# Where softmax's division is done in a cross-attention: after the values by transposed reciprocals, or on the exponentials ahead of their transposes

## The chip, the cores and the metric

The kernel runs on one core of a Trainium2 chip. The time is device time in microseconds from one execution of the whole program; several executions are made, and their median is compared. The profile is of one further execution.

## What is computed

The network has two layers on `x` (16 batches of 256 rows of 256 features) with a context of the same shape. Each layer is a cross-attention and a mixture of experts, each added to `x` after a layer norm. The change is in the second layer's cross-attention ("Layer 1" in the code, which counts from 0), 16 heads of 64:

```python
xn = _layernorm(x, ln_gamma, ln_beta)
q = (xn @ w_q).reshape(B, SQ, NUM_HEADS, DIM_HEAD)
k, v = jnp.split(context @ w_kv, 2, axis=-1)      # both (B, SK, heads, 64)
scores = jnp.einsum('bqhd,bkhd->bhqk', q * SCALE, k)
attn = jax.nn.softmax(scores, axis=-1)
out = jnp.einsum('bhqk,bkhd->bqhd', attn, v).reshape(B, SQ, INNER)
out = out @ w_out + b_out
return out * jnp.tanh(gate[0])
```

All is float32.

## The kernel before

Four stages follow each other: Layer 0's attention, its experts, Layer 1's attention (`layer1_attention`, L869), its experts. The page's lines are mostly L58, the line of the helper that records every instruction, so instructions are told apart by the tiles they name.

In Layer 1's attention a batch has 256 queries and 256 keys. The work is cut into units of two heads: eight units (`s` = 0 to 7) a batch, 128 in all. Of one unit, with `p` for the head, `lt` for the half of the queries and `mc` for the half of the keys:

- `l1_logits` (L938): four matmuls write `lg`; VectorE takes the maxima over keys, negated, into `nmx`, in two reductions.
- `l1_exp` (L956): ScalarE's exponentials, two for `lt` = 0 and two for `lt` = 1, write `ex` and add up the sums in `den`.
- `l1_transposes` (L974): eight TensorE transposes of `ex`, evicted into `exT` by VectorE (`mc` = 0) and ScalarE (`mc` = 1).
- `l1_sums` (L966): VectorE takes the reciprocals of the sums (`rden`); GpSimd spreads each over 64 columns (`wide`).
- `l1_scale` (L985): two TensorE transposes of `wide` into half of the bank `ov`, and a ScalarE copy of them into `scale`. Thus every output feature of a head has its queries' reciprocals in its own row.
- `l1_values` (L996): four matmuls of `exT` and the values into the other half of `ov`; VectorE multiplies by `scale` while it evicts into `oT`.

Logits and exponentials are of the current unit, and the others of the unit before it (`last`), which is one step behind.

Between these parts each step fills in pieces of other work, named in `places` by the unit's number: `p+1` is the next batch's projections (`l1_prepare`, L1050: keys, values, queries, and in unit 5 also the transposes of the normalised input, scaled into `xnT` by VectorE), `f-1` is the output projection of the batch before (`l1_finish`, L1121, in units 1 and 2, with the residual `up` and the statistics of the next norm), and `i+2` the input of the batch after the next (`l1_input`, L1013: gathers of the experts' outputs in unit 0, two additions and statistics in each of units 3 and 4, normalisation and more statistics in unit 5, the second normalisation in unit 6). A step has two fillers for TensorE, one ahead of the transposes and one behind them; the first is evicted by ScalarE and the second by VectorE (`self.side`). In the last batches, where no next batch is left, `choices` (L1176), the routing of the last stage, takes the place of `p+1`.

Every engine's instructions go out in the order in which the program names them (`in_order`, L105): an instruction that waits holds up all that is behind it on its engine. PSUM has two buffers for `lg`, three banks for `ps`, which transposes and projections take in turn, and one buffer for `ov`.

Of the kernel before, what the change touches and what calls it, by code (L numbers as in the profile page):

```python
# [8 lines left out]
F32 = mybir.dt.float32  # L9
I32 = mybir.dt.int32  # L10
AF = mybir.ActivationFunctionType
ALU = mybir.AluOpType
# [3 lines left out]
P = 128  # L16
B, S, D = 16, 256, 256
# [4 lines left out]
H = 16  # L22
DH0 = 16
DH1 = 64
# [39 lines left out]
class Net:  # L64
# [804 lines left out]
    def layer1_attention(self, mv2, mv3, late):  # L869
        nc, tc = self.nc, self.tc  # L870
        with ExitStack() as ctx:
            self.ps_lg = ctx.enter_context(tc.tile_pool(name="c_lg", bufs=2, space=PSUM, reuse_waits="tile"))
            self.ps = ctx.enter_context(tc.tile_pool(name="c_ps", bufs=3, space=PSUM, reuse_waits="tile"))
            self.ps_ov = ctx.enter_context(tc.tile_pool(name="c_ov", bufs=1, space=PSUM, reuse_waits="tile"))
            keep = ctx.enter_context(tc.tile_pool(name="c_keep", bufs=1, reuse_waits="tile"))
            self.work = ctx.enter_context(tc.tile_pool(name="c_work", bufs=2, reuse_waits="tile"))
            self.small = ctx.enter_context(tc.tile_pool(name="c_small", bufs=4, reuse_waits="tile"))

            self.pick_tiles(late)
            self.mv2, self.mv3 = mv2, mv3  # L880
            self.rs2 = keep.tile([P, NT], F32, name="ln2_rs")
            self.mvi, self.rsi = self.stats_tiles(keep, "ln2i")
            self.tg = keep.tile([P, 1], F32, name="tg")
            nc.scalar.activation(self.tg, self.gate, AF.Tanh)

            self.l1 = {b: {} for b in range(B)}
            pieces = {
                "i": {b: self.l1_input(b) for b in range(B)},
                "p": {b: self.l1_prepare(b) for b in range(B)},
                "f": {b: self.l1_finish(b) for b in range(B)},  # L890
            }
            nothing = iter(())

            places = (
                ("p+1", "p+1", "i+2"), ("f-1", "f-1", ""), ("f-1", "f-1", ""),
                ("p+1", "p+1", "i+2"), ("p+1", "p+1", "i+2"), ("p+1", "p+1", "i+2"),
                ("p+1", "p+1", "i+2"), ("p+1", "p+1", ""),
            )  # L900

            first = {0: "i+1", 1: "i+1", 2: "i+1", 3: "i+1 i+2", 4: "i+1 i+2"}
            choices = self.choices()

            def go_on(b, words):
                for word in words.split():
                    at = b + int(word[1:])
                    if word[0] == "p" and at >= B:

                        next(choices, None)  # L910
                    else:
                        next(pieces[word[0]].get(at, nothing), None)

            self.in_order()
            last = None
            for b in range(-1, B + 1):
                for s in range(H // 2):
                    one, two, chain = places[s]
                    if b < 0:
                        chain = first.get(s, "i+2")  # L920
                    self.l1_sums(last)
                    unit = self.l1_logits(b, s) if 0 <= b < B else None
                    self.l1_exp(unit, 0)
                    self.side = self.s
                    go_on(b, one)
                    self.l1_transposes(last)
                    self.l1_exp(unit, 1)
                    self.l1_scale(last)
                    go_on(b, chain)
                    self.side = self.v  # L930
                    go_on(b, two)
                    self.l1_values(last)
                    last = unit
            for _ in choices:
                pass
            self.any_order()
# [26 lines left out]
                bias=unit["nmx"][:, lt, p : p + 1], accum_out=unit["den"][:, lt, p : p + 1],  # L963
            )

    def l1_sums(self, unit):  # L966
        if unit is None:
            return
        rden = self.small.tile([P, 2, 2], F32, tag="rden", name="rden")
        self.v.reciprocal(rden, unit["den"])  # L970
        unit["wide"] = wide = self.small.tile([P, 2, 2, DH1], F32, tag="wide", name="wide", bufs=2)
        self.g.tensor_copy(wide, rden.unsqueeze(3).to_broadcast([P, 2, 2, DH1]))

    def l1_transposes(self, unit):  # L974
        if unit is None:
# [6 lines left out]
                    self.tp(tr[:, p, lt, :], unit["ex"][:, p, lt, ts(mc, P)])  # L982
            self.evac(exT[:, mc], tr.rearrange("p h t l -> p h (t l)"), on=(self.v, self.s)[mc])

    def l1_scale(self, unit):  # L985

        if unit is None:
            return

        unit["ov"] = ov = self.ps_ov.tile([P, 2, S], F32, tag="ov", name="ov")  # L990
        for lt in range(2):
            self.tp(ov[:, 1, ts(lt, P)], unit["wide"][:, lt].rearrange("p h d -> p (h d)"))
        unit["scale"] = scale = self.small.tile([P, S], F32, tag="scale", name="scale", bufs=2)
        self.s.copy(scale, ov[:, 1, :])

    def l1_values(self, unit):  # L996
        if unit is None:
            return
        t, s = self.l1[unit["b"]], unit["s"]
        if s == 0:  # L1000
            t["oT"] = []
        oT = self.work.tile([P, S], F32, tag="oT", name="oT", bufs=11)
        t["oT"].append(oT)
        ov, h0 = unit["ov"], 2 * s % (H // 2)
        for mc in range(2):
            for p in range(2):
                self.mm(
                    ov[ts(p, DH1), 0, :], t["vv"][2 * s // (H // 2)][:, mc, ts(h0 + p, DH1)],
                    unit["exT"][:, mc, p, :], start=(mc == 0), stop=(mc == 1),
                )  # L1010
        self.v.tensor_tensor(oT, ov[:, 0, :], unit["scale"], ALU.mult)

    def l1_input(self, b):  # L1013

# [465 lines left out]
```

## Time and profile before

| | us |
|---|---|
| median of 3 runs | 2285.07 |
| lowest and highest | 2281.6, 2285.92 |
| the profiled execution, its own time | 2289.61 |
| its span, first to last instruction | 2287.6 |
| Layer 1's attention, first logits to last | about 906 (1186 to 2092) |

The page gives the busy time of each engine, and for groups of instructions the mean time of one and what ended the idle time ahead of them. PE is TensorE's matmuls, PEld its weight loads (which run ahead of the matmuls and often show the wait), DVE is VectorE, ACT is ScalarE and POOL is GpSimd. In a timeline the columns are the start, the busy time, the engine, the line, the operation with the tiles it writes and reads, and in brackets the idle time of the engine just before with what ended it. Successive instructions of one kind stand as one row with their number; a matmul's listed time is longer than its distance to the next, since they are pipelined.

### The profile page before, as it was taken

What the parts mean: (1) busy time and instruction counts of PE and PEld (TensorE: products, weight loads), DVE (VectorE), ACT (ScalarE), POOL (GpSimd) and SP (SyncE); (2) the same over time, 40 slices, a digit from 0 to 9 for tenths busy, and PEclk for the clock granted to TensorE, in tenths of its full rate; (3) what the DMA queues carried; (4) which work ended last, traced back from release to release, by engine and by line L of the source; (5) the groups of instructions that cost most, each with busy time, mean ns of one, the idle gap of its engine ahead of it and who ended that gap; (6) DMA issues with size and microseconds to landing.
All of it is one profiled execution on the core that took longest, in us unless ns stands there. A gap on an engine that the chain in (4) does not pass through costs nothing. (4 is left out here: it accounts for less than half of the span.)

```text
span 2287.6 us, 40849 instructions
## 1 busy us (share of the span) xinstructions
PE 2138.9 (93%) x15742; PEld 1633.6 (71%) x15742; DVE 1169.1 (51%) x2692; ACT 920.7 (40%) x3092; POOL 399.2 (17%) x581
## 2 busy tenths in 40 slices
PE   6889989988589999999979999999999999998998
PEld 4666666666378998998856666666666666666887
DVE  4778787887510110110135555555555555547445
ACT  2656555555222222222214444444444444444432
POOL 2232333322300000000021111111111111016200
PEclk9999999999789999999989999999999999999999
DMA  9910000000077777777510000000000000002112
GB/s 371 422 45 13 19 15 15 19 12 18 25 231 251 251 231 255 249 229 259 173 33 10 10 10 10 10 10 10 10 10 10 10 10 10 1 1 85 32 39 75
DMA packets 129025, 200.42 MB, mean 88 GB/s; under 512 B 14480, under 2 KB 107040, under 8 KB 124480
## 3 DMA queue, kind: packets, MB, share of 16 engines
q1 hardware_dynamic: 120880, 176.14, 22.7%
q0 software_dynamic: 7136, 21.12, 2.8%
q8 instruction: 124, 2.03, 0.4%
q14 instruction: 69, 0.57, 0.1%
q10 hardware_dynamic: 816, 0.56, 0.1%
HBM read 142.35 MB, written 55.44 MB: 86 GB/s over the span
## 5 line engine op out<-in xcount | busy, mean ns | idle before, releaser
L58 ACT ACTIVATE ex<-lg,nmx 128x256 f32<-128x256 f32 x1024 | 473.9, 476 | 723.9 <-DVE nmx L58 723.8
L58 DVE TENSOR_REDUCE nmx<-lg 128x2 f32<-128x512 f32 x512 | 329.0, 685 | 110.6 <-PE lg L58 109.0
L58 PE MATMUL tr<-ident,ex 128*128 128x128 f32 x2048 | 280.0, 278 | 26.0 <-DVE exT L58 24.2
L58 PEld LDWEIGHTS tr<-ident,ex 128*128 128x128 f32 x2048 | 237.2, 143 | 77.6 <-DVE exT L58 41.1
L796 ACT ACTIVATE hT<-ph,b 128x256 f32<-128x256 f32 (+1 forms) x368 | 131.7, 423 | 367.9 <-issue 290.5
L58 PE MATMUL ph<-xT,w 128*128 128x256 f32 (+1 forms) x1472 | 257.9, 334 | 0.8 <-DVE xT L779 0.8
L58 PE MATMUL py<-w,hT 128*128 128x256 f32 x1136 | 252.8, 379 | 0.0
L58 PEld LDWEIGHTS ph<-xT,w 128*128 128x128 f32 x1472 | 232.1, 192 | 23.6 <-DVE xT L779 1.2
L58 DVE COPY exT<-tr 128x512 f32<-128x512 f32 x256 | 169.5, 683 | 130.6 <-PE tr L58 130.6
L58 PEld LDWEIGHTS py<-w,hT 128*128 128x128 f32 x1136 | 212.3, 190 | 27.0
L58 PE MATMUL lg<-kT,qT 32*128 32x256 f32 (+1 forms) x2048 | 224.1, 410 | 1.7 <-ACT ex L58 1.7
L58 PE MATMUL ov<-exT,vv 128*32 128x256 f32 (+1 forms) x2048 | 215.5, 399 | 7.1 <-ACT scale L58 5.2
L58 ACT ACTIVATION_READ_ACCUMULATOR ex<-lg,nmx 128x1 f32 x1024 | 212.0, 207 | 0.0
L58 POOL COPY wide<-rden 128x256 f32<-128x256 f32 x160 | 63.7, 398 | 821.5 <-DVE rden L58 462.5
L58 PEld LDWEIGHTS lg<-kT,qT 32*128 32x128 f32 (+1 forms) x2048 | 137.5, 190 | 87.5 <-issue 77.2
L58 PEld LDWEIGHTS ov<-exT,vv 128*32 128x32 f32 (+1 forms) x2048 | 90.7, 124 | 102.9 <-ACT scale L58 48.6
L58 POOL DMA_INDIRECT yg<-ys,row_out x64 | 62.7, 980 | 518.6 <-PE mm L58 497.7
L58 ACT ACTIVATE exT<-tr 128x512 f32<-128x512 f32 x256 | 147.3, 608 | 14.2 <-PE tr L58 12.3
L779 DVE COPY xT<-tr 128x512 f32<-128x512 f32 (+1 forms) x46 | 26.2, 570 | 242.0 <-PE tr L58 242.0
L811 DVE TENSOR_TENSOR yo<-py,b 128x512 f32<-128x512 f32 (+1 forms) x46 | 26.2, 570 | 226.0 <-PE py L58 208.4
L58 PE MATMUL mm<-xnT,w_q 128*128 128x256 f32 x512 | 129.3, 397 | 6.1 <-DVE xnT L58 6.1
L58 PE MATMUL mm<-w_kv,ctxT 128*128 128x512 f32 x256 | 127.5, 621 | 3.6 <-DVE vv L58 3.5
(201 smaller groups left out, 2697.7 us busy)
## 6 DMA issues: line engine op xcount, KB each, us to landing
w<-in_L_W SPq DMA_DIRECT2D x92, 1024.0 KB, 7.1
xs<-zero SPq DMA_DIRECT2D x4, 8192.0 KB, 52.6
xg<-xs SPq DMA_DIRECT2D x25, 256.0 KB, 5.5
ys<-yo SPq DMA_DIRECT2D x25, 256.0 KB, 6.8
b<-in_L_b SPq DMA_DIRECT2D x46, 128.0 KB, 4.2
x<-in_x SPq DMA_DIRECT2D x16, 256.0 KB, 6.0
ctxT<-in_ctxT SPq DMA_DIRECT2D x16, 256.0 KB, 6.0
w<-in_L_W1T SPq DMA_DIRECT2D x8, 512.0 KB, 9.1
```

The source lines that it names most:

```text
L58: self.last = f(*args, **kw)
L779: self.v.tensor_copy(s["xT"][:, :, 0 : s["rows"]], tr.rearrange("p c t l -> p c (t l)"))
L796: self.s.activation(s["hT"][:, h0 + j, 0:rows], ph[:, j, :], AF.Gelu, bias=s["b1"][:, h0 + j : h0 + j + 1],)
L811: self.v.tensor_tensor(yo[:, 0:nt, :], py, s["b2"].unsqueeze(1).to_broadcast([P, nt, D]), ALU.add)
```

## The change

The exponentials are divided by their sums before they are transposed. `l1_sums` and `l1_scale` are gone, and with them the tile `wide`, its two transposes and the copy `scale`. A new function, `l1_divide`, is called twice a unit, once for each half of the queries: VectorE takes the reciprocals of two sums and multiplies the two pieces of `ex` in place, each by its column. The values then need no scaling, and ScalarE copies them into `oT`.

```diff
-                    self.l1_sums(last)
                     unit = self.l1_logits(b, s) if 0 <= b < B else None
                     self.l1_exp(unit, 0)
                     self.side = self.s
                     go_on(b, one)
                     self.l1_transposes(last)
                     self.l1_exp(unit, 1)
-                    self.l1_scale(last)
+                    self.l1_divide(unit, 0)
                     go_on(b, chain)
+                    self.l1_divide(unit, 1)
                     self.side = self.v
                     go_on(b, two)
                     self.l1_values(last)
...
-    def l1_sums(self, unit):
+    def l1_divide(self, unit, lt):
+
         if unit is None:
             return
-        rden = self.small.tile([P, 2, 2], F32, tag="rden", name="rden")
-        self.v.reciprocal(rden, unit["den"])
-        unit["wide"] = wide = self.small.tile([P, 2, 2, DH1], F32, tag="wide", name="wide", bufs=2)
-        self.g.tensor_copy(wide, rden.unsqueeze(3).to_broadcast([P, 2, 2, DH1]))
+        rden = self.small.tile([P, 2], F32, tag="rden", name="rden")
+        self.v.reciprocal(rden, unit["den"][:, lt, :])
+        for p in range(2):
+            ex = unit["ex"][:, p, lt, :]
+            self.v.tensor_scalar(ex, ex, rden[:, p : p + 1], None, ALU.mult)
...
-    def l1_scale(self, unit):
...
-        unit["ov"] = ov = self.ps_ov.tile([P, 2, S], F32, tag="ov", name="ov")
-        for lt in range(2):
-            self.tp(ov[:, 1, ts(lt, P)], unit["wide"][:, lt].rearrange("p h d -> p (h d)"))
-        unit["scale"] = scale = self.small.tile([P, S], F32, tag="scale", name="scale", bufs=2)
-        self.s.copy(scale, ov[:, 1, :])
...
-        ov, h0 = unit["ov"], 2 * s % (H // 2)
+        ov, h0 = self.ps_ov.tile([P, S], F32, tag="ov", name="ov"), 2 * s % (H // 2)
...
-        self.v.tensor_tensor(oT, ov[:, 0, :], unit["scale"], ALU.mult)
+        self.evac(oT, ov, on=self.s)
```

More of the change, by code (lines that the diff above doesn't have):

```diff
@@ L983, in l1_transposes @@
             self.evac(exT[:, mc], tr.rearrange("p h t l -> p h (t l)"), on=(self.v, self.s)[mc])
-    def l1_scale(self, unit):
-        if unit is None:
-            return
-        unit["ov"] = ov = self.ps_ov.tile([P, 2, S], F32, tag="ov", name="ov")
-        for lt in range(2):
-            self.tp(ov[:, 1, ts(lt, P)], unit["wide"][:, lt].rearrange("p h d -> p (h d)"))
-        unit["scale"] = scale = self.small.tile([P, S], F32, tag="scale", name="scale", bufs=2)
-        self.s.copy(scale, ov[:, 1, :])
     def l1_values(self, unit):
@@ L1007, in l1_values @@
                 self.mm(
-                    ov[ts(p, DH1), 0, :], t["vv"][2 * s // (H // 2)][:, mc, ts(h0 + p, DH1)],
+                    ov[ts(p, DH1), :], t["vv"][2 * s // (H // 2)][:, mc, ts(h0 + p, DH1)],
                     unit["exT"][:, mc, p, :], start=(mc == 0), stop=(mc == 1),
                 )
-        self.v.tensor_tensor(oT, ov[:, 0, :], unit["scale"], ALU.mult)
+        self.evac(oT, ov, on=self.s)
     def l1_input(self, b):
```

## The prediction

> **What bounds the kernel now.** I read the page first, then the busy time by stretches, then the groups of instructions of the stretch that the change touches, and last the timeline of single units of that stretch.
>
> ```profile
> PE 2138.9 (93%) x15742; PEld 1633.6 (71%) x15742; DVE 1169.1 (51%) x2692; ACT 920.7 (40%) x3092; POOL 399.2 (17%) x581
> ```
>
> TensorE is the busy engine. The page's chain that ended last covers 3% of the span, so it can't carry an argument about Layer 1. One steady batch of Layer 1 lies between two projections of logits, at 1469.11 and 1525.68:
>
> ```profile
> 1469.11:1525.68 56.57, 56.56 (x327) 39.04 (x325) 33.16 (x72) 24.57 (x86) 9.00 (x16) 1.00 0.04 10
> ```
>
> In 56.57 us PE is busy throughout, VectorE for 33.16 and ScalarE for 24.57, at a granted clock of 1.00. This invites the thought that whatever leaves PE shortens the batch. The timeline of unit 6 (of 8, two heads each) says otherwise:
>
> ```profile
> 1511.51 1.13 PE L58 MATMUL lg<-kT,qT 64*128 64x256 f32 x8
> 1512.57 1.99 PE L58 MATMUL mm<-xnT,w_q 128*128 128x256 f32 x8
> 1512.69 1.29 DVE L58 TENSOR_REDUCE nmx<-lg 128x2 f32<-128x512 f32 x2 [0.49 <-PE lg L58]
> 1514.10 0.47 ACT L58 ACTIVATE ex<-lg,nmx 128x256 f32<-128x256 f32 x1 [4.34 <-DVE nmx L58]
> 1514.40 1.04 PE L58 MATMUL tr<-ident,ex 128*128 128x128 f32 x8
> 1515.01 0.59 ACT L58 ACTIVATE qT<-mm 128x512 f32<-128x512 f32 x1
> 1515.28 0.38 PE L58 MATMUL ov<-ident,wide 128*128 128x128 f32 x2
> 1515.65 1.59 PEld L58 LDWEIGHTS mm<-xnT,w_q 128*128 128x128 f32 x8 [0.23 <-ACT qT L58]
> 1515.65 1.99 PE L58 MATMUL mm<-xnT,w_q 128*128 128x256 f32 x8
> ```
>
> The two transposes of reciprocals (`ov<-ident,wide`) stand between the transposes of exponentials and the second projection, and the second projection waits for ScalarE's eviction of the first: of the three banks of `ps`, it takes the one that the eviction frees. From the logits to it: 1.18 to the maxima, 1.41 to the exponentials, 0.91 to the eviction, 0.64 to the projection, 4.14 us. PE's own work, 1.06 + 1.83 + 0.88 + 0.22, would be done at 3.99. Units 1 and 2, whose filler is the output projection (one bank, no eviction in between), show the transposes' true price:
>
> ```profile
> 1479.96 0.38 PE L58 MATMUL ov<-ident,wide 128*128 128x128 f32 x2
> ...
> 1480.18 1.89 PE L58 MATMUL mm<-w_out,oT 128*128 128x256 f32 x8
> ```
>
> There the next matmul starts 0.22 us after them, and the unit takes 6.82 instead of 7.08.
>
> **Part by part.** *Removed on PE: two transposes a unit.* The group's mean of 274 ns each is latency; start to start two cost 0.22. In units 0, 3, 4, 5, 6 and 7 they stand under the 4.14 us and are worth nothing; in 1 and 2, 0.22 each. [...]
>
> *Removed on ScalarE: the copy `scale` (0.39), replaced by the copy of `oT`* behind the values; ScalarE idles some 4 us a unit ahead of the exponentials (4.34 above), so this costs nothing. One thing is gained: the first exponential waits for two semaphores in the changed program where it waited for three. The trace's records of ScalarE have both forms: 117 ns from the end of the maxima with two held ahead of it (123 in Layer 1), 95 with one (48 in Layer 0). So 0.02 a unit on the 4.14 us chain.
>
> *Removed on GpSimd: `wide` (0.40).* Off the path in steady batches; it matters once, below.
>
> *Added on VectorE: two divides a unit, each a reciprocal and two 128x256 multiplications by a column in SBUF; removed: one reciprocal and the product `oT` (0.42).* The nearest rows are exact twins:
>
> ```profile
> 545.40 0.68 DVE L58 TENSOR_REDUCE first<-key 128x2 f32<-128x512 f32 x1
> 546.11 0.62 DVE L58 TENSOR_SCALAR hot<-rev,first 128x256 f32<-128x256 f32 x2
> 546.64 0.18 DVE L58 TENSOR_TENSOR r_one<-hits,r_row 128x32 f32<-128x32 f32 x1
> ```
>
> The pair behind a dependent small result starts 0.03 after it and holds the engine for 0.53 (546.64 - 546.11). One alone:
>
> ```profile
> L58 DVE TENSOR_SCALAR hot<-rev,first 128x256 f32<-128x256 f32 x32 | 9.9, 351 | 0.6
> ```
>
>  With the reciprocal (166 ns at 128x2, row `r_sm`) a divide occupies 0.17 + 0.03 + 0.53 = 0.74. The bounds of a multiplication: 0.18, what the 128x32 product above costs with hardly any elements in it, and 0.48 from the row `x<-yg,gates,x`, which works on the same 256 elements with a column as well. I take 351, the row of the same instruction.
>
> [...] The trace starts the second of a pair 0.27 after the first, though each is listed at 0.35. [...] The row is of this engine and this shape: I keep it.
>
> *Where the divides stand.* The first is behind the copy `exT`, the second behind the chain pieces. It waits for the sums of the second pair of exponentials (there 5.5 after the logits); behind it in VectorE's queue are the second eviction or the residual, and then the next maxima. The next unit's transposes wait for the divided tile, but only 2.9 after the next logits. Units 0 and 7: free long before the next maxima (at 6.9 of 8.26). Units 3 and 4: 4.13 (free behind `exT`) + 0.74 + 1.6 (chain: two adds, statistics) + 0.74 + 0.61 = 7.8, before the next maxima at 8.26. Units 1 and 2: the sums are there at 5.5; divide to 6.26, then residual and statistics, 1.54, to 7.8; the next maxima could start at 6.60 + 1.18 = 7.78. Just fits. Unit 5 doesn't:
>
> ```profile
> 1507.52 0.69 DVE L58 COPY exT<-tr 128x512 f32<-128x512 f32 x1 [1.05 <-PE tr L58]
> 1508.13 0.40 DVE L58 TENSOR_SCALAR xn<-x,ln_mv,ln_rs 128x256 f32<-128x256 f32 x1
> ...
> 1510.77 0.99 DVE L58 TENSOR_SCALAR xnT<-tr,gamma,beta 128x256 f32<-128x256 f32 x2
> ```
>
> From its logits (1504.00): `exT` lets go at 4.13, divide to 4.87, the two normalisations with statistics (1508.13 to 1510.11, 1.98) to 6.85, divide to 7.59, eviction `vv` 0.61 to 8.20, `xnT` twice 0.455 to 9.11. Unit 6's maxima start at 9.11 instead of 8.69 (1512.69), and its first projection, which reads `xnT`, at 9.25 instead of 8.57. Its second projection is then due by ScalarE at 9.11 + 1.41 + 0.91 + 0.64 - 0.02 = 12.05, by PE at 9.25 + 1.83 + 0.88 = 11.96; before, 11.65. Unit 6 loses 0.4.
>
> *Sum.* A batch: -0.44 (units 1, 2) + 0.40 (unit 6) - 0.02 x 5 = -0.14, 15 times -2.1; the last batch has no unit-5 work: -0.5. Start of Layer 1: in batch 0 the values wait for ScalarE's `scale` for 3.05 and 2.20 us; they now wait only for `exT`, 1.2 earlier each, but unit 1's maxima stand behind two divides and an eviction, 1.26 later: -1.1. First unit of the last batch: PE waits 2.66 for GpSimd's normalised `xn`, which stood behind `wide`; now VectorE's half is last, at 2037.6 instead of 2038.57, and the second piece gains a little too: -1.2. Last unit: 0.22 and a GpSimd wait of 0.36: -0.6. In the last batch GpSimd normalises beside the divides; VectorE's own `xn` there takes 0.49 where it takes 0.41 alone: +0.4. Total -5.1 on the profiled 2289.61 (span 2287.6, 2.0 around it). The median of the runs is 4.5 lower, and the same difference is taken from it: 2280.0.
>
> **Rivals.** *PE is the bound and all its busy time counts:* 0.38 x 128 = 49 us, 2236. For it: 93%. Against: the ScalarE wait at every second projection. 3% for that, 7% for a gain of 8 to 15, if unit 6 isn't late (-6 more) or the chains are shorter than drawn. *VectorE's multiplication is dearer, and unit 5 decides:* each 0.1 on it falls four times on unit 6's maxima, and twice on unit 3's, whose slack is gone. At 481 ns that is 0.13 x 6 = 0.8 a batch, 12 us, less the 5: 2292. It ends above before from 0.055 more per multiplication, that is at 0.41. [...] Against: the twin row's spread of 346 to 354. 30%; a tenth of that would end inside what a measurement can tell. *The change doesn't do what it says:* the built order has 256 transposes fewer on PE and 512 multiplications more on VectorE, so no.
>
> **Numbers.** The walk as drawn has 60%, with a spread of some 4 us: 2276 to 2284. A measurement tells about 0.2%, 4.6 us, from no change; the walk's -5 lies at that border, so it gives 0.33 to faster and 0.27 to the same; with 0.10 of the rivals that gain and the dear multiplication (0.03 the same, 0.27 slower) that makes 0.43, 0.30 and 0.27. The range goes from the late unit 6 not appearing, 2273, to the dear multiplication, 2292.
>
> **What would show it.** `ex<-ex,rden` at 0.35 us; unit 6 at 7.5 and units 1 and 2 at 6.6 us from logits to logits; the others at 7.06; second projections still waiting for ScalarE, now with PE idle 0.39; PE's busy share lower by about two points. Wrong if ordinary units fall under 6.9 (then the eviction didn't bound them), if `ex<-ex,rden` is over 0.41, or if units 3 and 4 get longer.

## The result, and the profile after

| | before | after |
|---|---|---|
| median of 6 runs, us | 2285.49 | 2277.68 |
| lowest and highest | 2281.6, 2287.57 | 2274.13, 2281.92 |
| profiled execution, its span | 2289.61, 2287.6 | 2274.13, 2271.7 |
| first to last logits of Layer 1's attention, profiled execution | 899.13 | 888.60 |

The ratio is 0.997, with a 95% interval of 0.9956 to 0.9985: between 3.4 and 10.1 us faster, 7.8 by the medians, where 5.1 was forecast. (The 906 given above for before ran to 2092; its last logits start at 2085.15.)

The two profiled executions differ by 15.9 us in span, which is not the change's worth. 5.9 of them lie ahead of Layer 1's first logits (1186.02 and 1180.16), in stages that the change doesn't touch; in all ten profiles of this study these logits stand between 1180.16 and 1186.2, and after has the earliest. From the first logits to the last after gains 10.53; behind them it loses 0.5. This last stage is untouched as well, apart from the last unit at its head, and it also varies, from 202.45 to 207.0 over the ten profiles. After's profiled execution is also the fastest of its six, and the granted clock goes with that. Its mean over an execution was 0.980 in this one and 0.976 in before's profiled one, while after's six average 0.977, as 39 later executions of before do. Among those 39, the six at 0.980 took 2280.03 to 2283.44 and the eight at 0.975 took 2287.78 to 2289.97: an estimate of 1.4 us for each 0.001. So the 7.8 of the medians is a gain at about equal clock, and the difference of the two traces isn't.

On the page of after, the engines' busy time and the row of the new instruction:

```profile
PE 2104.4 (93%) x15486; PEld 1598.0 (70%) x15486; DVE 1276.8 (56%) x3204; ACT 941.0 (41%) x3092; POOL 351.1 (15%) x453
...
L58 DVE TENSOR_SCALAR ex<-ex,rden 128x256 f32<-128x256 f32 x512 | 158.9, 353 | 9.1
```

TensorE lost 34.5 us of busy time (2138.9 to 2104.4), VectorE took on 107.7, and the kernel is some 8 us faster: neither number gives the third. A steady batch of after, from logits to logits, shows why; the columns are the stretch and its length, the busy time of PE, PEld, DVE, ACT and POOL, the granted clock, the DMA share and GB/s:

```profile
1458.39:1514.81 56.42, 54.92 (x310) 37.20 (x308) 39.91 (x104) 25.88 (x86) 5.97 (x8) 1.00 0.04 10
```

PE was busy for 56.56 of 56.57 before, and is now for 54.92 of 56.42: of 1.64 us less work 0.15 became time, and 1.49 became waiting. By units (logits to logits, from the timelines):

| unit | 0 | 1 | 2 | 3 | 4 | 5 | 6 | 7 | batch |
|---|---|---|---|---|---|---|---|---|---|
| before | 7.08 | 6.82 | 6.82 | 7.07 | 7.08 | 7.51 | 7.08 | 7.09 | 56.57 |
| after | 7.07 | 6.61 | 6.61 | 7.07 | 7.07 | 7.49 | 7.45 | 7.06 | 56.42 |

Units 1 and 2 gain their two transposes, the others nothing, and unit 6 loses 0.37. Unit 6 of after, in the timeline:

```profile
1500.29 1.13 PE L58 MATMUL lg<-kT,qT 64*128 64x256 f32 x8
1500.37 0.68 DVE L58 COPY vv<-mm 128x512 f32<-128x512 f32 x1
...
1500.97 0.98 DVE L58 TENSOR_SCALAR xnT<-tr,gamma,beta 128x256 f32<-128x256 f32 x2
1501.56 0.30 PEld L58 LDWEIGHTS mm<-xnT,w_q 128*128 128x128 f32 x2 [0.53 <-DVE xnT L58]
...
1501.88 1.27 DVE L58 TENSOR_REDUCE nmx<-lg 128x2 f32<-128x512 f32 x2
1502.01 1.16 PEld L58 LDWEIGHTS mm<-xnT,w_q 128*128 128x128 f32 x6 [0.16 <-DVE xnT L58]
...
1503.25 0.47 ACT L58 ACTIVATE ex<-lg,nmx 128x256 f32<-128x256 f32 x1 [2.46 <-DVE nmx L58]
```

The maxima carry no bracket: VectorE went to them straight from `xnT`. They start 1.59 after the logits, where an ordinary unit's start at 1.18, and the exponentials follow 1.37 behind them. In the ordinary units the eviction's wait is still there, with 0.20 where the prediction looked for 0.39:

```profile
1496.28 0.59 ACT L58 ACTIVATE vv<-mm 128x512 f32<-128x512 f32 x1
...
1496.92 0.30 PEld L58 LDWEIGHTS mm<-w_kv,ctxT 128*128 128x128 f32 x2 [0.44 <-ACT vv L58]
1496.92 1.98 PE L58 MATMUL mm<-w_kv,ctxT 128*128 128x512 f32 x4 [0.20 <-ACT vv L58]
```

(The bracket counts from the listed end of the transposes. They start at 1495.68, and in units 1 and 2 the next matmul follows 0.87 after their start; counted from there, PE waits 0.37.) The steady part gave only 1.9 us, over batches 1 to 14. The rest of the 10.53 is at the edges: 4.84 in batch 0 and 3.80 in the last batch.

**Start of Layer 1.** PE's rows of before, units 1 and 2 of batch 0:

```profile
1196.49 1.98 PE L58 MATMUL ov<-exT,vv 128*64 128x256 f32 x8 [3.05 <-ACT scale L58]
1198.39 2.08 PE L58 MATMUL lg<-kT,qT 64*128 64x256 f32 x8
...
1204.66 1.30 PE L58 MATMUL ov<-exT,vv 128*64 128x256 f32 x8 [2.20 <-ACT scale L58]
```

and of after, unit 2:

```profile
1191.31 1.13 PE L58 MATMUL lg<-kT,qT 64*128 64x256 f32 x8
1192.37 1.09 PE L58 MATMUL tr<-ident,ex 128*128 128x128 f32 x8
1194.52 0.65 PE L58 MATMUL ov<-exT,vv 128*64 128x256 f32 x4 [1.05 <-DVE exT L58]
```

The waits for `scale` are gone, as forecast; what is left are waits for the divided `ex` and for `exT`, of 0.80, 1.62 and 1.05. But the same eight matmuls of logits took 2.08 before and take 1.13. Units 1 and 2 as stretches, before and then after:

```profile
1190.73:1198.39 7.66, 4.61 (x27) 2.50 (x26) 2.64 (x5) 4.22 (x17) 0.39 (x1) 0.79 0.00 1
1198.39:1205.89 7.50, 5.30 (x28) 3.49 (x26) 2.40 (x5) 2.68 (x10) 0.40 (x1) 0.73 0.00 0
```

```profile
1184.88:1191.31 6.43, 3.66 (x26) 1.95 (x25) 4.73 (x13) 3.69 (x15) 0.00 (x0) 1.00 0.00 1
1191.31:1196.02 4.71, 3.39 (x27) 1.97 (x25) 3.45 (x9) 2.70 (x11) 0.00 (x0) 1.00 0.00 0
```

The granted clock (third column from the right) was 0.79 and 0.73, and is 1.00. The prediction had taken the rows' slow durations as fixed and moved only the wait.

But the shorter waits alone did not ensure the full clock. The kernel with unit 5 relieved (below) has the same instructions up to unit 5 of batch 0, and the same waits. In its profile the clock did fall, to one half for 6.82 us; two stretches, and the row with the longest wait:

```profile
1191.86:1195.28 3.42, 1.47 (x10) 0.87 (x8) 2.81 (x8) 0.68 (x5) 0.00 (x0) 1.00 0.00 0
1195.28:1202.10 6.82, 6.16 (x26) 3.50 (x28) 3.87 (x10) 3.50 (x13) 0.00 (x0) 0.50 0.00 0
```

```profile
1195.75 2.12 PE L58 MATMUL ov<-exT,vv 128*64 128x256 f32 x8 [1.63 <-DVE exT L58]
```

and in after it did not:

```profile
1185.37:1188.78 3.41, 1.93 (x14) 1.08 (x12) 2.79 (x8) 1.06 (x5) 0.00 (x0) 1.00 0.00 0
1188.79:1192.20 3.41, 2.13 (x16) 1.08 (x16) 2.21 (x8) 2.69 (x10) 0.00 (x0) 1.00 0.00 0
```

```profile
1189.72 0.65 PE L58 MATMUL ov<-exT,vv 128*64 128x256 f32 x4 [1.62 <-DVE exT L58]
```

These stretches are steps of 3.41 us, counted from a change of the clock (the last section): in the kernel with unit 5 relieved from the one at 1195.28, in after from the one at 1175.13. There, the wait of 0.80 and most of the 1.63 fell into one step, in which PE was busy for 1.47. Here, a step's end cut the long wait in two, and PE was busy for 1.93 and 2.13. Units 1 and 2 took 12.55 there and 11.14 here, so 1.4 of the 4.84 is luck of this execution.

**Last batch.** Its first unit waits for the normalised input of the last stage. The wait in PE's rows, in before and then in after:

```profile
2038.57 1.12 PE L58 MATMUL tr<-ident,xn 128*128 128x128 f32 x4 [2.66 <-POOL xn L58]
```

```profile
2025.04 0.55 PE L58 MATMUL tr<-ident,xn 128*128 128x128 f32 x3 [1.45 <-DVE xn L58]
```

The unit as a stretch, in before and then in after:

```profile
2034.78:2044.27 9.49, 6.68 (x41) 5.32 (x39) 4.72 (x11) 3.92 (x12) 7.11 (x10) 0.82 0.00 1
```

```profile
2022.19:2028.83 6.64, 5.19 (x38) 3.67 (x36) 4.01 (x11) 3.89 (x12) 2.88 (x4) 1.00 0.00 0
```

The wait fell from 2.66 to 1.45, the 1.2 that the prediction had, and the clock rose from 0.82 to 1.00, which it had not: 2.85 us in all. Here the two go together throughout: the clock fell in the three profiles of this study with the wait of 2.66, and in none of the seven with 1.45 or 1.46.

### The profile page after: what moved, and what is told of

It is laid out like the page before. It is cut to its first block, busy times and chain, and to the rows that moved or that the text cites. A ratio compares the mean times of both kernels' runs of the same rounds, so it can differ in the third digit from the quotient of the medians.

```text
span 2271.7 us, 40451 instructions
## 1 busy us (share of the span) xinstructions
PE 2104.4 (93%) x15486; PEld 1598.0 (70%) x15486; DVE 1276.8 (56%) x3204; ACT 941.0 (41%) x3092; POOL 351.1 (15%) x453
## 5 line engine op out<-in xcount | busy, mean ns | idle before, releaser
L58 DVE TENSOR_SCALAR ex<-ex,rden 128x256 f32<-128x256 f32 x512 | 158.9, 353 | 9.1
```

What stands on the lines that cost most here:

```text
L58: self.last = f(*args, **kw)
```

## The experiments

The theory: an ordinary unit is bound by ScalarE's eviction, which frees the third bank of `ps`; unit 6 by VectorE's queue of unit 5; the edges by waits of PE that also lower its clock. The rivals: PE's work bounds every unit; the divides take back in every unit what the transposes gave.

**No divides.** Both calls of after are taken out, so the exponentials stay undivided.

```diff
-                    self.l1_divide(unit, 0)
                     go_on(b, chain)
-                    self.l1_divide(unit, 1)
```

> The changed kernel with both divides left out, so the exponentials go undivided: the removals alone. My theory (second projections wait for ScalarE's eviction of the first): units 1 and 2 stay at 6.61, the other ordinary units at 7.06, unit 5 at 7.49, and unit 6 falls from 7.45 to 7.06; a steady batch 56.0 us instead of 56.42. Rival (PE is the bound, and the divides' load on VectorE hides a gain): without them the ordinary units fall to 6.7, a batch to 53.8.

Measured: 2273.13 against 2287.03 of before, ratio 0.9941 (0.9917 to 0.9964). Units 7.09, 6.61, 6.61, 7.08, 7.09, 7.51, 7.09, 7.09, a batch of 56.15. Unit 3 of this kernel:

```profile
1477.87 1.13 PE L58 MATMUL lg<-kT,qT 64*128 64x256 f32 x8
...
1482.02 1.98 PE L58 MATMUL mm<-w_kv,ctxT 128*128 128x512 f32 x4 [0.23 <-ACT vv L58]
1484.94 1.13 PE L58 MATMUL lg<-kT,qT 64*128 64x256 f32 x8
```

With neither the transposes nor the divides an ordinary unit still takes 7.08 and still waits for `vv`. So the divides hold up no ordinary unit; in a steady batch they cost 0.27, with 0.36 in unit 6 and nothing in the others, which are 0.01 to 0.02 longer without them. With transposes left out of a stage in which PE had looked wholly busy, the gain is 0.42 a batch and not 8 times 0.22.

**Unit 5 relieved.** The normalisations of unit 5 go to unit 6, and those of unit 6 to unit 7; the divides stay.

```diff
-                ("p+1", "p+1", "i+2"), ("p+1", "p+1", "i+2"), ("p+1", "p+1", "i+2"),
-                ("p+1", "p+1", "i+2"), ("p+1", "p+1", ""),
+                ("p+1", "p+1", "i+2"), ("p+1", "p+1", "i+2"), ("p+1", "p+1", ""),
+                ("p+1", "p+1", "i+2"), ("p+1", "p+1", "i+2"),
```

> The changed kernel with the normalisation of the batch after next moved from unit 5 to unit 6, and its second part from unit 6 to unit 7. My theory (VectorE's queue in unit 5 is too long, and xnT comes late): unit 6 falls from 7.45 to 7.06, all others stay; a steady batch 56.0 instead of 56.42, 6 us in all. Rival (unit 6 is late because of VectorE's total load, or of the divides in unit 6): the lateness moves along to unit 7 or stays, batch 56.4.

Measured: 2274.30 against 2287.03, ratio 0.9944 (0.9922 to 0.9966). Unit 6 is at 7.06, a batch at 56.04. Unit 6's timeline:

```profile
1505.50 0.99 DVE L58 TENSOR_SCALAR xnT<-tr,gamma,beta 128x256 f32<-128x256 f32 x2
1506.09 1.13 PE L58 MATMUL lg<-kT,qT 64*128 64x256 f32 x8
...
1507.28 1.29 DVE L58 TENSOR_REDUCE nmx<-lg 128x2 f32<-128x512 f32 x2 [0.79 <-PE lg L58]
```

`xnT` is written ahead of the logits, and the maxima follow 1.19 after the logits, as in an ordinary unit, with VectorE idle for 0.79 ahead of them. The queue of unit 5 was the cause of the late unit 6.

**Its control: the same move in before.**

> The kernel before with the normalisation moved from units 5 and 6 to 6 and 7, as in the run on the changed kernel. A control: my theory (only with the divides in the queue is unit 6 late) leaves every unit as it is, batch 56.57, same time. Rival (the move is a gain by itself): units 5 or 6 shorten here too.

Measured: 2285.06 against 2285.29, ratio 0.9993 (0.9981 to 1.0006); all units of a steady batch within 0.02 of before's. The move itself is worth nothing; it pays only where the divides have used up VectorE's spare time.

**Four banks.** `ps` gets a fourth bank and the values take theirs from it, so no PSUM is added; the second projection no longer needs the bank that ScalarE is emptying.

```diff
-            self.ps = ctx.enter_context(tc.tile_pool(name="c_ps", bufs=3, space=PSUM, reuse_waits="tile"))
-            self.ps_ov = ctx.enter_context(tc.tile_pool(name="c_ov", bufs=1, space=PSUM, reuse_waits="tile"))
+            self.ps = ctx.enter_context(tc.tile_pool(name="c_ps", bufs=4, space=PSUM, reuse_waits="tile"))
...
-        ov, h0 = self.ps_ov.tile([P, S], F32, tag="ov", name="ov"), 2 * s % (H // 2)
+        ov, h0 = self.bank([P, S], "ov"), 2 * s % (H // 2)
```

> The changed kernel with the buffer of ov given to the pool ps: four banks in turn, ov among them, so the second projection takes a bank that ScalarE's eviction of the same unit does not hold. My theory: the wait goes, ordinary units fall from 7.07 to 6.70, units 1 and 2 stay at 6.60, unit 5 7.13, unit 6 rises to 7.8 because xnT is late by more; a steady batch 54.9, 24 us in all. Rival (the chain from maxima to exponentials bounds the unit in another way than by the bank): units stay at 7.07.

Measured: 2244.98 against 2287.03, ratio 0.9815 (0.9794 to 0.9837). Units 6.61, 6.61, 6.61, 6.59, 6.61, 7.02, 7.30, 6.61, a batch of 53.93. The ordinary unit falls by 0.46, below the 6.70 that was expected. An ordinary unit's second projection:

```profile
1456.23 0.59 ACT L58 ACTIVATE kT<-mm 128x512 f32<-128x512 f32 x1
...
1456.52 1.89 PE L58 MATMUL mm<-ctxT,w_kv 128*128 128x256 f32 x8
```

It starts while ScalarE is still evicting the first (to 1456.82), and it is listed at 1.89 where after has 1.99: in after the weight load waits for `vv` too (0.44, above) and starts with the matmul, at 1496.92, and in after's unit 1, where nothing is waited for, it starts 0.11 ahead of it (1469.11 and 1469.22). The 0.46 is the wait of 0.37 and, by an estimate from these rows, this 0.1. Unit 6 is less late than expected (7.30 for 7.8).

**Both: four banks, and unit 5 relieved.**

> Both of the last two edits. My theory: ordinary units 6.70, unit 5 7.13, unit 6 6.70; a steady batch 53.8 us, 42 us in all against the kernel before. Rival (with PE no longer waiting, VectorE's queue becomes the bound and the maxima start late): units at 7.0 and more, a batch of 55 or over.

Measured: 2231.64 against 2287.03, ratio 0.976 (0.9738 to 0.9781), faster than both kernels: 55 us below before, 46 below after by the medians of two sessions. Unit 6 in its timeline:

```profile
1490.07 0.59 ACT L58 ACTIVATE qT<-mm 128x512 f32<-128x512 f32 x1
...
1490.26 1.60 PEld L58 LDWEIGHTS mm<-xnT,w_q 128*128 128x128 f32 x8
1490.36 1.89 PE L58 MATMUL mm<-xnT,w_q 128*128 128x256 f32 x8
```

A batch of it as a stretch:

```profile
1446.57:1499.80 53.23, 53.23 (x310) 37.12 (x308) 39.73 (x105) 25.87 (x86) 5.41 (x8) 1.00 0.03 9
```

The projection starts at 1490.36, while ScalarE is still evicting the one before it (to 1490.66). Now PE is the bound. The fully busy line (53.23 of 53.23, at the clock of 1.00) can't show this by itself, since before had one too. But no row of PE's matmuls has a bracket in this batch, and all units but one take 6.59 to 6.61, as long as units 1 and 2, whose second projection never waited; unit 5's 7.02 has the transposes of the normalised input on top. Before with four banks was not run; with its `scale` in the other half of `ov`, it isn't the same edit.

**Every multiplication twice.** After, with a second multiplication of each piece by a column of ones.

```diff
         for p in range(2):
             ex = unit["ex"][:, p, lt, :]
             self.v.tensor_scalar(ex, ex, rden[:, p : p + 1], None, ALU.mult)
+        for p in range(2):
+            ex = unit["ex"][:, p, lt, :]
+            self.v.tensor_scalar(ex, ex, self.one[:, 0:1], None, ALU.mult)
```

> The changed kernel with every divided piece multiplied once more by a column of ones, so each divide holds VectorE for 1.27 us instead of 0.74. My theory (VectorE has slack in units 0, 1 and 7 and none in 2 to 6): unit 3 rises to about 7.7, unit 4 to 7.2, unit 5 to 8.0, unit 6 to 8.1, units 0, 1, 2 and 7 stay; a steady batch 58.3 us, some 28 us more than the changed kernel and 20 more than the kernel before. Rival (VectorE at 59% of a steady batch has room for it): under 57, about the time of the kernel before.

Measured: 2309.56 against 2285.29, ratio 1.0103 (1.0074 to 1.0131). Units 7.06, 6.61, 6.61, 7.59, 7.12, 8.00, 7.98, 7.06, a batch of 58.02 to 58.31. Unit 3's second projection in the timeline:

```profile
1496.17 1.98 PE L58 MATMUL mm<-w_kv,ctxT 128*128 128x512 f32 x4 [0.74 <-ACT vv L58]
```

The unit as a stretch:

```profile
1491.50:1499.09 7.59, 6.85 (x34) 3.47 (x32) 6.79 (x21) 3.29 (x11) 0.00 (x0) 1.00 0.01 2
```

The wait is still named ScalarE's, but it has grown from 0.22 to 0.74 because the maxima, two steps ahead of it, came late, 1.76 after the logits for 1.18: VectorE is busy for 6.79 of 7.59. The forecast's losing rival is thus real in its mechanism, and in its price: a pair more holds VectorE for 0.53, and it appears once in unit 3 (+0.52) and twice in units 5 and 6 together (+1.04). VectorE's cover ends in units 3 to 6, and units 0, 1, 2 and 7 have room for twice the multiplications.

**`scale` early, in before.** ScalarE copies `scale` ahead of the second pair of exponentials, so that the values of batch 0 come sooner with nothing else changed.

```diff
-                    self.l1_exp(unit, 1)
                     self.l1_scale(last)
+                    self.l1_exp(unit, 1)
```

> The kernel before with the copy scale moved ahead of the second pair of exponentials on ScalarE; nothing else. It asks for the gain at the start of Layer 1. My theory (in batch 0 the values wait for scale, PE idles and its clock is lowered): units 1 to 3 of batch 0 shorten from 7.66, 7.50 and 8.18 to about 6.7, 6.5 and 7.3, and the granted clock there rises from 0.77; steady batches stay at 56.57; 3 us in all. Rival (the lower clock has nothing to do with this wait): unit 3 stays at 8.18, and 1 and 2 fall by 0.9 at most.

Measured: 2282.42 against 2285.29, ratio 0.9983 (0.9969 to 0.9997). Batch 0 falls from 56.81 to 53.30 (units 4.71, 6.75, 5.99, 7.07), against -4.84 in after. Two stretches of its batch 0, the first from within unit 0 to the start of unit 3, the second in unit 3:

```profile
1185.00:1201.00 16.00, 11.83 (x71) 7.80 (x71) 5.86 (x13) 9.08 (x30) 0.79 (x2) 0.89 0.00 1
1201.00:1208.00 7.00, 6.99 (x36) 3.63 (x34) 4.59 (x11) 3.18 (x11) 0.40 (x1) 1.00 0.01 2
```

The waits for `scale` are 2.13 and 2.03 here instead of 3.05 and 2.20, and the clock is back at 1.00 by unit 3, where before had 0.82. It stood at one half for 3.41 us of the batch, where before had 10.24. So shorter waits, 1.1 in sum, and the clock that came with them give 3.5 us in this profile; the clock's part is of one execution. One thing went against expectation: the first unit of the last batch rose from 9.49 to 10.70. Its wait for `xn` is the same 2.66, and PE's granted clock in the unit is 0.68 where before had 0.82: it stood at one half for 6.83 us instead of 3.41. The wait reached 0.73 us into the first of these low steps, and 0.33 in before; the last section has what followed the other low steps of before.

**`wide` on VectorE, in before.** The copy of the reciprocals moves off GpSimd.

```diff
-        self.g.tensor_copy(wide, rden.unsqueeze(3).to_broadcast([P, 2, 2, DH1]))
+        self.v.tensor_copy(wide, rden.unsqueeze(3).to_broadcast([P, 2, 2, DH1]))
```

> The kernel before with wide spread by VectorE instead of GpSimd. It asks for the gain at the start of the last batch. My theory (GpSimd's normalised xn stood behind wide): unit 0 of the last batch falls from 9.49 to about 8; steady batches stay within 0.3 of 56.57, since VectorE has 0.4 spare ahead of the maxima. Rival (GpSimd isn't what unit 0 waits for): it stays at 9.5.

Measured: 2290.97 against 2285.29, ratio 1.0026 (1.0018 to 1.0035). The first unit of the last batch falls from 9.49 to 7.14, with the wait that after has:

```profile
2036.30 0.55 PE L58 MATMUL tr<-ident,xn 128*128 128x128 f32 x3 [1.46 <-DVE xn L58]
```

So `wide` in GpSimd's queue was what held up the normalised input there. Steady unit 3 rises by 0.19 (7.07 to 7.26), a batch by 0.18. By the trace, Layer 1 is then 0.3 shorter in sum (898.81), yet the kernel is 5.7 slower by the medians. In its profile the last stage takes 205.8 where before had 202.5, with the clock at 0.83 in stretches where before had 0.91; the edit doesn't reach this stage. The clock explains a part at most: its mean is 0.975 over this kernel's 20 executions and 0.977 over before's 39, an estimate of some 3 us by the 1.4 per 0.001 above. How this, or the rest, follows from the edit, or whether it does, stays open.

## Why the prediction was right, and where its steps were not

- *Units 1 and 2, -0.22 each.* 6.82 to 6.61: right.
- *Ordinary units bound by ScalarE's eviction, transposes worth nothing there.* 7.08 to 7.07: right. The unit doesn't fall without divides, and it falls by 0.46 with a fourth bank. The rival of 2236, that all of PE's busy time counts, falls by both. It was wrong for this kernel's three banks only: with four, PE is the bound.
- *Unit 6, +0.4.* 7.08 to 7.45; the maxima at 9.08 after unit 5's logits for 9.11 forecast. The first projection was drawn too late, at 9.25; it starts at 8.76, because its first matmuls read only the first half of `xnT` (the waits of 0.53 and 0.16 above). That did no harm, since ScalarE's branch of the walk was the later one, as it said. Where the branch through PE decides, with four banks, the same error showed as 7.30 for 7.8.
- *The multiplication at 351 ns and a pair at 0.62.* 353 and 0.62. The second piece of a pair starts 0.27 after the first in after too, though each is listed at 0.35. 509 of the 512 lie under 375 ns.
- *A steady batch, -0.14.* -0.15: right.
- *Start of Layer 1, -1.1, and the batch's own -0.1.* Measured -4.84. The mis-sized term is the duration of PE's rows: they were taken from before, where the clock was 0.79, 0.73 and 0.82 in units 1 to 3. With shorter gaps the low clock went too, in this profile; with the same gaps and the lower clock of the run with unit 5 relieved it would have been -3.4. PE's busy time in these three units fell from 18.09 to 13.89, and only some 1.2 of that is the listed time of the transposes left out (0.38 to 0.44 a unit).
- *The last batch, -0.5, -1.2 and +0.4.* Measured -3.80. In the first unit the wait was right and the clock was left out (-2.85). Units 3 to 6 gained 0.11 to 0.16 each, where the +0.4 had been counted: there, too, the values had waited for ScalarE's `scale` (in unit 3 of before it ends at 2063.66, and they start at 2063.72).
- *The last unit, -0.6.* From the last logits to the first output projection 12.28 became 11.88, -0.4.

The sum was near by its steady part and too small at both edges: -10.5 from first to last logits and -0.4 in the last unit, for -5.1. The medians say -7.8, in an interval that reaches to -10.1, some 3 us less than the trace's sum. A part of that is the better clock of after's profiled execution, of which 1.4 shows in batch 0; the other stages vary as well, and no run here settles how the rest divides. PE's busy share, forecast to fall by about two points, fell by one, from 93.5 to 92.6. That 2280.0 lies so near to 2277.68 thus owes something to luck: the mechanism of the steady part held, and both edges were mis-sized, in large part by the clock.

## What to carry to other kernels

A fully busy engine in a stretch can still be waiting in it, as long as pipelined work hides the wait in its listed time (before: PE busy for 56.56 of 56.57, with a weight load that waited 0.23 for ScalarE): find the instruction whose bracket names another engine, and ask what frees its buffer before counting work as time. When VectorE takes on work that was hidden elsewhere, walk its queue unit by unit; here one unit of eight had no room, and moving two pieces of filler by one unit gave back all of it. And durations read in a stretch with a low granted clock are no constants (the logits of batch 0 took 2.08 at one half and 1.13 at the full clock): a change that shortens the gap can change them too, and one profile of it is one draw.

## What the runs showed of the hardware

- PE's granted clock reads 1.00 or 0.50 in every record of the traces of before and after (30 and 26 of them); the means of 0.73 to 0.82 that before has above mix the two. At 0.50, logits that take 1.13 took 2.08. In each of these two traces all changes lie whole multiples of 3.41 us apart (before: low from 1195.14 to 1201.97, and from 1205.38 to 1208.80), and from trace to trace these steps lie differently against the program: unit 1 of batch 0 starts 1.00 ahead of the next step in before (1190.73 and 1191.73) and 0.49 in after (1184.88 and 1185.37).
- The longest single gap does not decide: 1.62 left the clock at 1.00 in after, and 1.63 did not with unit 5 relieved. The idle share of a step tells more. In Layer 1 of before and after PE was idle for at most 0.43 of each step at full clock that was followed by another (518 of them), and for 0.50, 0.64 and 0.68 of the three that were followed by the half, all of before. Outside Layer 1 the two overlap: in before a step with 0.40 (at 225.76) was followed by the half, and one with 0.48 (at 2106.51) by the full clock. So what decides isn't shown. Of the steps at the half in Layer 1 of before, the three with idle shares of up to 0.10 were followed by the full clock (0.10 at the last batch's wait), and the one with 0.39 by another half, as was the one with 0.21 with `scale` early. PE's listed ends are modelled, so these shares are rough.
- The last stage, which is the same in all kernels of this study, took between 202.45 and 207.0 us, with the clock at 0.83 to 0.91 in some stretches, which differed between profiles. A change in one stage can thus be masked by 3 us in another (205.8 with `wide` on VectorE for 202.5 in before).
- In after's ordinary units the weight load of the second projection waited for ScalarE as the matmul did (0.44 and 0.20 to 1496.92). With four banks and no wait an ordinary unit came out 0.1 us below what the wait alone was worth (6.61 for 6.70), and its second projection is listed at 1.89 for 1.99.
- Two of the 512 multiplications took 584 and 605 ns, both with a GpSimd instruction in progress (an indirect DMA, and a normalisation of 1.23). Of the 512, 102 had one beside them; the others of these were not slowed so, and what sets the two apart isn't shown.
